# A two-layer graph network on one core: the second layer's preparation spread over 27 units, its first weight factor on ScalarE, and f1, f2 taken from the turning products

## The chip, the core and the metric

The kernel runs on one core of a Trainium2 chip. The metric is the device time of one execution in microseconds. The kernel before takes 3600.33 us in the median of three runs (3599.05 to 3604.43); the profiled execution spans 3601.0 us.

## What is computed

Sixteen graphs of N = 1024 nodes with F = 256 features pass through two layers. Each layer ends with a residual sum and a layer norm. Layer 0 is an attention layer with batch norms and is not touched here. Layer 1, for each of H = 4 heads, is

```
fts    = inputs @ W[h]
f1, f2 = fts @ w1[h] + b1[h], fts @ w2[h] + b2[h]
logits = f1[:, None] + f2[None, :]
coefs  = a*softmax(leaky_relu(logits, 0.2) + bias_mat) + (1-a)*softmax(adj)
out    = elu(coefs @ fts + bias[h] + inputs)
x      = layernorm(inputs + mean of out over heads)
```

`bias_mat` is -1e9 where there is no edge, so the first softmax needs only neighbours. The exponential of a leaky ReLU of a sum is the larger of two products: exp(f1 + f2) and exp(0.2 (f1 + f2)). Divided by exp(0.2 f1), which cancels in the softmax, a weight is max(exp(0.8 f1) exp(f2), exp(0.2 f2)): `A` holds the first factor per target row, and two columns behind the features in each source row's table hold the other two.

## The kernel before, in words

Layer 0 runs first, up to 799.4 us. It leaves the hidden features turned around, features over partitions, in `h_dram`. The adjacency stands in `adj16` as bf16.

Layer 1 uses that most columns of the adjacency are empty in a given block of 128 rows. Per graph the nodes are in K = 8 blocks. For each block `it` of target rows the used source nodes are collected into chunks of 128; `CAPS` says how many chunks each block may need (6, 4, 3, 3, 3, 3, 2, 2, together 26). A chunk's feature rows `xc` and mask columns `mc` are fetched by indirect DMA from GpSimd's queue. `weights` makes the 128 x 128 weights of the four heads from them, and PE multiplies.

Two things are therefore done per graph:

*Preparation* (class `Graph`). `load_mask`, `load_h`, `load_x` bring the data in. `counts`, `used`, `places`, `placed`, `mark`, `pick`, `indices` find which source goes to which chunk. `elu`, `turn`, `residual`, `means`, `norm`, `scale` finish layer 0's output and its layer norm. `shares1` multiplies `h` with `WW` to give f1 and f2, and `factors` makes their exponentials. `table` and `spread` write the row table and the factors of f1 to DRAM. `split`, `total`, `mask`, `neighbours`, `summed`, `shares` make the second softmax, which has only two values per row, from a plain product with the adjacency (block `mr` per row block, in `fp32r`).

*Units* (class `Unit`), 16 per graph, one for a row block and a pair of heads. `gather` (PE, L1389) multiplies chunks into `pu`; `share` (ScalarE) starts `s` with the second softmax; `mix` (DVE, L1405 to L1409) adds the first; `turn` and `turned` transpose `s` (PE, then ScalarE); `linear` (PE, L1429) multiplies by W1 into `pv`; `addends` (GpSimd, L1376) adds bias and input; `add`, `exps`, `sum`, `power`, `close` finish with the ELU, the mean over heads and the layer norm.

The order within each engine is the order in which the Python code calls these steps, since everything is inside `tc.manual_schedule()`: there is no planner, and each engine works through its queue in order. The main loop runs over `n`, and calls for each `n` the steps of units at fixed distances behind (`linear` of unit n - 2, `mix` of n - 1, `add` of n - 3). Preparation steps are hung into this loop by `side(g)`: `first[i]` runs just ahead of `mix`, `after[i]` at the end of unit i, mostly while the graph before computes its units. A step's PE part stands in `first[i]` and its DVE part in `after[i]` of the same unit, as here:

```
first[8] += [g.pick, g.shares1]
after[8] += [g.indices, g.factors]
```

Graph 0's preparation has no units to stand beside and is written out ahead of the loop. Buffers matter for the steps below: `pv` (L1426) has one PSUM buffer, `pu` two, the preparation's PSUM tag `s` two, the chunks' `xc` and `mc` 17 each.

Of the kernel before, what the change touches and what calls it, by code (L numbers as in the profile page):

```python
# [8 lines left out]
F32 = mybir.dt.float32  # L9
# [10 lines left out]
P = 128  # L20
# [7 lines left out]
def kernel(  # L28
# [83 lines left out]
    mt_dram = [dpool.tile([N + 1, N], BF16, name=f"mt_dram_{i}") for i in range(2)]  # L112
# [16 lines left out]
    with tc.tile_pool(name="ipool", bufs=1) as ipool:  # L129
# [14 lines left out]
        for i in range(2):  # L144
            nc.gpsimd.dma_start(xe_dram[i][N : N + 1, :], zero[:, 0:XW])
            nc.gpsimd.dma_start(mt_dram[i][N : N + 1, :], zero)
# [890 lines left out]
    with ExitStack() as l1:  # L1037
        xpool = l1.enter_context(tc.tile_pool(name="x1pool", bufs=2))
# [5 lines left out]
        ps_s = l1.enter_context(tc.tile_pool(name="ps_s", bufs=2, space=PSUM))  # L1044

        class Graph:
# [7 lines left out]
            def load_mask(self):  # L1054

                b = self.b
                if b in ready1:
                    self.mt = ready1[b]
                else:
                    self.mt = m1pool.tile([P, K, N], BF16, tag="mt", name=f"mt1_{b}")  # L1060
                    nc.sync.dma_start_transpose(self.mt, adj16[b])
                self.rw = pk.tile([P, K, N], BF16, tag="rw", name=f"rw_{b}", bufs=1)
                nc.sync.dma_start(self.rw, adj16[b].rearrange("(q p) j -> p q j", p=P))
# [14 lines left out]
            def counts(self):  # L1078

                self.pc = ps_s.tile([P, K, K], F32, tag="s", name=f"pc_{self.b}")  # L1080
                for k in range(K):
                    for q in range(K):
                        nc.tensor.matmul(
                            self.pc[:, k, q : q + 1], self.rw[:, q, k * P : (k + 1) * P],
                            ones16[:, 0:1], start=True, stop=True,
                        )

            def used(self):

                self.act = pk.tile([P, K, K], BF16, tag="act", name=f"act_{self.b}", bufs=2)  # L1090
                nc.vector.tensor_scalar(self.act, self.pc, 1.0, None, ALU.min)
# [14 lines left out]
            def placed(self):  # L1106

                b = self.b
                pos = pk.tile([P, K + 1, K], F32, tag="pos", name=f"pos_{b}", bufs=1)
                nc.scalar.copy(pos, self.pp)  # L1110
                nc.vector.tensor_tensor(most, most, pos[:, K, :], ALU.max)
                pi = pk.tile([P, K, K], I32, tag="pi", name=f"pi_{b}", bufs=1)
                nc.vector.tensor_copy(pi, pos[:, 0:K, :])
                nc.vector.tensor_scalar(pi, pi, P - 1, None, ALU.bitwise_and)
                self.r16 = pk.tile([P, K, K], FP16, tag="r16", name=f"r16_{b}", bufs=2)
                nc.vector.tensor_copy(self.r16, pi.rearrange("p k q -> p q k"))
                nc.vector.tensor_tensor(pos[:, 0:K, :], pos[:, 0:K, :], pi, ALU.subtract)
# [3 lines left out]
                    t, pos[:, 0:K, :].rearrange("p k q -> p (k q)").unsqueeze(2).to_broadcast([P, K * K, n]),  # L1121
# [7 lines left out]
                self.oh = pk.tile([P, K, P, K], FP16, tag="rw", name=f"oh_{b}", bufs=1)  # L1129

            def mark(self, q):
                nc.vector.tensor_tensor(
                    self.oh[:, q], iota16, self.r16[:, q, :].unsqueeze(1).to_broadcast([P, P, K]),
                    ALU.is_equal,
                )

            def pick(self):

                self.pl = ps_s.tile([P, NC], F32, tag="s", name=f"pl_{self.b}")
                n = max(CAPS)  # L1140
                for q in range(K):
                    for k in range(K):
                        nc.tensor.matmul(  # L1143
                            self.pl[:, CAT[q] : CAT[q] + CAPS[q]],
                            self.oh[:, q, :, k], self.t16[:, k, q * n : q * n + CAPS[q]],
# [3 lines left out]
            def store_mask(self):  # L1149
                nc.sync.dma_start(  # L1150
                    mt_dram[self.b % 2][0:N, :].rearrange("(k p) i -> p k i", p=P), self.mt
                )

            def indices(self):

                b = self.b
                self.ix = pk.tile([P, NC], U32, tag="ix", name=f"ix_{b}", bufs=2)
                self.im = pk.tile([P, NC], U32, tag="im", name=f"im_{b}", bufs=2)
                nc.vector.tensor_scalar(self.ix, self.pl, float(N), None, ALU.add)
                nc.vector.scalar_tensor_tensor(self.im, self.pl, float(K), row8, ALU.mult, ALU.add)  # L1160

            def fetch_rows(self, c):

                self.xc[c] = pk.tile([P, XW], F32, tag="xc", name=f"xc_{self.b}_{c}", bufs=17)
# [5 lines left out]
            def fetch_mask(self, c):  # L1170

                self.mc[c] = pk.tile([P, P], BF16, tag="mc", name=f"mc_{self.b}_{c}", bufs=17)
                nc.gpsimd.indirect_dma_start(  # L1173
                    out=self.mc[c], out_offset=None,
                    in_=mt_dram[self.b % 2].rearrange("n (q i) -> (n q) i", i=P),
# [10 lines left out]
            def weights(self, c):  # L1186

                it = max(q for q in range(K) if CAT[q] <= c)
                w = self.w[c] = pk.tile([P, H, P], F32, tag="w", name=f"w_{self.b}_{c}", bufs=12)
                xc = self.xc[c]  # L1190
                for h in range(H):
                    nc.vector.tensor_scalar(  # L1192
                        w[:, h, :], self.A[it][:, h, :], xc[:, F1 + h : F1 + h + 1],
                        xc[:, F1 + H + h : F1 + H + h + 1], ALU.mult, ALU.max,
                    )
                nc.vector.tensor_tensor(  # L1196
                    w, w, self.mc[c].unsqueeze(1).to_broadcast([P, H, P]), ALU.mult
                )

            def elu(self, oc):  # L1200

                hv = self.h[:, oc, :]
                m = pk.tile([P, N], F32, tag="hm", name=f"hm_{self.b}_{oc}", bufs=1)
                nc.scalar.activation(
                    m, hv, AF.Exp, bias=t3[:, oc : oc + 1], scale=s3[:, oc : oc + 1]
# [4 lines left out]
                nc.vector.scalar_tensor_tensor(hv, m, 1.0, hv, ALU.min, ALU.max)  # L1210

            def turn(self, k):
                pz = self.pz[k] = ps_s.tile([P, F], F32, tag="s", name=f"pz_{self.b}_{k}")
                for oc in range(C):
                    nc.tensor.transpose(
                        pz[:, oc * P : (oc + 1) * P], self.h[:, oc, k * P : (k + 1) * P], ident
                    )

            def residual(self, k):
                xk = self.x[:, k, 0:F]  # L1220
                nc.vector.tensor_tensor_reduce(
                    out=xk, in0=self.pz[k], in1=xk, scale=1.0, scalar=0.0,
                    op0=ALU.add, op1=ALU.add, accum_out=self.mv[:, 0, k : k + 1],
                )

            def shares1(self):

                self.pf = ps_s.tile([P, K, 2 * H], F32, tag="s", name=f"pf_{self.b}")
                for k in range(K):
                    for oc in range(C):  # L1230
                        nc.tensor.matmul(  # L1231
                            self.pf[:, k, :], self.h[:, oc, k * P : (k + 1) * P], WW[:, oc, :],
                            start=(oc == 0), stop=(oc == C - 1),
                        )

            def means(self):

                nc.vector.tensor_scalar(self.mv[:, 0], self.mv[:, 0], -1.0 / F, None, ALU.mult)
                for k in range(K):
                    d = pk.tile([P, F], BF16, tag="d", name=f"d_{self.b}_{k}", bufs=2)  # L1240
# [4 lines left out]

            def norm(self):
                self.rs = pk.tile([P, 3, K], F32, tag="rs", name=f"rs_{self.b}", bufs=2)
                rs = self.rs
                nc.vector.tensor_scalar(self.mv[:, 1], self.mv[:, 1], 1.0 / F, None, ALU.mult)
                inv_std(rs[:, 1, :], self.mv[:, 1, :], rs[:, 0, :])  # L1250
                nc.vector.tensor_tensor(rs[:, 2, :], self.mv[:, 0], rs[:, 1, :], ALU.mult)
# [8 lines left out]
            def factors(self):  # L1260
# [3 lines left out]
                nc.vector.tensor_tensor(self.f, self.pf, xw[:, b], ALU.add)  # L1264
# [6 lines left out]
                f2 = self.f[:, :, H : 2 * H]  # L1271
                nc.vector.memset(self.x[:, :, F : F + 1], 1.0)
                nc.scalar.activation(self.x[:, :, F1 : F1 + H], f2, AF.Exp)
# [12 lines left out]
            def split(self, k):  # L1286

                if k == 0:
                    self.xs = pk.tile([P, K, 2, F2], F32R, tag="xs", name=f"xs_{self.b}", bufs=1)
                    nc.vector.memset(self.xs[:, :, 0, F:F2].bitcast(F32), 1.0)  # L1290
                xk = self.x[:, k, 0:F]
                nc.scalar.copy(self.xs[:, k, 0, 0:F], xk)
                nc.vector.tensor_tensor(  # L1293
                    self.xs[:, k, 1, 0:F], xk, self.xs[:, k, 0, 0:F].bitcast(F32), ALU.subtract
                )

            def total(self):

                b = self.b
                px = ps_s.tile([P, F], F32, tag="s", name=f"pX_{b}")  # L1300
                for k in range(K):
                    for part in range(2):
# [3 lines left out]
                        )  # L1306
                self.X = pk.tile([P, F], F32, tag="X", name=f"X_{b}", bufs=2)
                nc.scalar.copy(self.X, px)
                self.deg = pk.tile([P, K], F32, tag="deg", name=f"deg_{b}", bufs=2)

            def mask(self, it):

                self.mr[it] = pk.tile([P, K, P], F32R, tag="mr", name=f"mr_{self.b}_{it}", bufs=3)
                nc.gpsimd.dma_start(self.mr[it], self.mt[:, :, it * P : (it + 1) * P])  # L1314
# [14 lines left out]
            def summed(self, it):  # L1329
                b, pm = self.b, self.pm[it]  # L1330
                self.S[it] = pk.tile([P, F], F32, tag="S", name=f"S_{b}_{it}", bufs=K + 1)
# [333 lines left out]
```

## Time and profile before

| stretch, us from the start | what it holds | length |
|---|---|---|
| 0 to 799.4 | layer 0 | 799.4 |
| 799.4 to 913.9 | graph 0's preparation, to the first `mix` | 114.5 |
| 913.9 to 1075.7 | graph 0's units | 161.8 |
| 1075.7 to 3484.2 | units of graphs 1 to 14, each with the next one's preparation | 14 x 172.0 |
| 3484.2 to 3601.0 | units of graph 15 | 116.8 |

A stretch begins with the first L1405 of a graph: DVE runs that line once per unit. Over the whole span PE is busy for 78%, DVE for 77%, GpSimd for 39% and ScalarE for 37%. Where two engines are each busy for four fifths and neither is full, the average doesn't tell what bounds: one has to ask, inside one such stretch, who waits for whom. A group of the profile gives busy time and the mean duration of one instruction; because instructions of one engine overlap, the distance from start to start is often shorter than the duration. An fp32 product on PE appears as two records, a transpose as one.

### The profile page before, as it was taken

Reading aid. Unit: us, or ns where it says so; the run is one execution under the profiler, and the core shown is the slowest. Engines: PE = TensorE matmul, PEld = TensorE weight load, DVE = VectorE, ACT = ScalarE, POOL = GpSimd, SP = SyncE. Lnnn points to the kernel's source line nnn. Section 1 sums busy time; section 2 is a strip of 40 time slices with the busy share of each in tenths; the row PEclk is TensorE's granted clock in tenths of the full one; section 3 lists DMA queues with packets and bytes.
Section 4 is the critical chain, followed back from the end, with each engine's and each line's share of the span. In section 5 each row is a group of like instructions: output and inputs, shape, how many; then the busy total and the mean of one; then the engine's idle time right before and its main releaser. Section 6 shows DMA issues by size and latency. Waiting matters only on the chain.

```text
span 3601.0 us, 45794 instructions
## 1 busy us (share of the span) xinstructions
PE 2810.2 (78%) x15591; PEld 2233.4 (62%) x15591; DVE 2777.1 (77%) x6820; ACT 1319.3 (37%) x2484; POOL 1392.6 (39%) x1425
## 2 busy tenths in 40 slices
PE   7936999985787777787877777787778787877786
PEld 6723444434676666675766666676667576766675
DVE  4369999953877878787878787868787877878788
ACT  1247777742233232333332323233333332332323
POOL 0010000004454545453535454454545454545462
PEclk9957999996887979898879888888888897989898
DMA  9797985537473746464646475655556564746441
GB/s 278 210 268 152 240 207 158 158 106 150 125 146 93 151 100 142 103 153 90 151 92 158 88 171 91 150 94 146 104 134 120 130 134 109 151 99 143 102 86 35
DMA packets 647283, 496.53 MB, mean 138 GB/s; under 512 B 286680, under 2 KB 567296, under 8 KB 640896
## 3 DMA queue, kind: packets, MB, share of 16 engines
q1 hardware_dynamic: 462656, 320.18, 32.1%
q0 software_dynamic: 183168, 170.81, 27.6%
q8 instruction: 127, 2.08, 0.2%
q10 hardware_dynamic: 1216, 2.51, 0.2%
q14 instruction: 116, 0.95, 0.1%
HBM read 291.09 MB, written 135.21 MB: 118 GB/s over the span
## 4 chain that ended last, share of the span: by engine, by line
DVE 32%; PE 12%; issue 9%; DMA 9%; POOL 6%; ACT 6%; SPq 2%; another core or an unknown queue 1%; DVEq 0%; POOLq 0%; ACTq 0%
DVE w L1192 8%; PE pv L1429 4%; DMA A<-a_dram 4%; DVE w L1196 3%; PE pf L1231 3%; DVE v L1436 3%; DMA mc<-mt_dram,im 2%; DVE s L1409 2%; DVE xs L1293 2%; POOL v L1376 2%; ACT d L1241 2%; POOL mc L1173 2%; PE pl L1143 2%; DVE v L1449 2%; DMA mr<-mt 2%
## 5 line engine op out<-in xcount | busy, mean ns | idle before, releaser
L1429 PE MATMUL pv<-W1s,sT 128*128 128x256 f32 x2048 | 659.2, 479 | 566.9 <-DVE z L1405 432.8
L1429 PEld LDWEIGHTS pv<-W1s,sT 128*128 128x128 f32 x2048 | 469.1, 238 | 716.7 <-issue 478.5
L1389 PE MATMUL pu<-xc,w 128*128 128x257 f32 x3328 | 821.2, 400 | 11.3 <-DVE w L1196 9.1
L1389 PEld LDWEIGHTS pu<-xc,w 128*128 128x128 f32 x3328 | 656.6, 204 | 104.9 <-DVE w L1196 12.2
L1192 DVE TENSOR_SCALAR w<-A,xc 128x128 f32<-128x128 f32 x1664 | 508.3, 376 | 54.0 <-DMA A<-a_dram 54.0
L1376 POOL TENSOR_TENSOR v<-x,bias 128x512 f32<-128x512 f32 x256 | 301.1, 1176 | 495.1 <-DVE acc L1447 311.0
L1165 POOL DMA_INDIRECT xc<-xe_dram,ix x416 | 417.9, 1005 | 144.0 <-issue 123.8
L1173 POOL DMA_INDIRECT mc<-mt_dram,im x416 | 426.0, 1024 | 104.9 <-issue 100.1
L584 PE MATMUL pa<-em,wh 128*128 128x512 f32 x1024 | 451.2, 598 | 18.9 <-issue 13.4
L584 PEld LDWEIGHTS pa<-em,wh 128*128 128x128 f32 x1024 | 193.5, 192 | 251.6 <-issue 235.7
L1472 ACT ACTIVATE o<-o,ors 128x256 f32<-128x256 f32 x128 | 76.8, 600 | 739.0 <-DVE ors L1469 556.6
L1440 ACT ACTIVATE m<-v,neg 128x512 f32<-128x512 f32 x256 | 184.8, 722 | 395.2 <-DVE z L1405 293.7
L1196 DVE TENSOR_TENSOR w<-w,mc 128x512 f32<-128x512 f32 x416 | 317.0, 762 | 14.2
L1324 PE MATMUL pm<-xs,mr 128*128 128x256 f32 (+1 forms) x2048 | 282.8, 294 | 36.0 <-DMA mr<-mt 35.6
L1324 PEld LDWEIGHTS pm<-xs,mr 128*128 128x128 f32 x2048 | 265.5, 196 | 43.6 <-issue 37.0
L1409 DVE SCALAR_TENSOR_TENSOR s<-pu,z,s 128x256 f32<-128x256 f32 x512 | 224.2, 479 | 22.3 <-ACT m L1440 0.5
L1399 ACT ACTIVATE s<-S,q 128x256 f32<-128x256 f32 x512 | 228.3, 493 | 1.2 <-DVE q L1350 1.2
L1423 ACT COPY sT<-pt 128x512 f32<-128x512 f32 x256 | 147.5, 576 | 121.2 <-PE pt L1417 119.0
L1463 POOL TENSOR_TENSOR ors<-ors,mhalf 128x1 f32<-128x1 f32 x128 | 72.8, 569 | 300.3 <-DVE ors L1469 284.6
L1314 POOL DMA_DIRECT2D mr<-mt x128 | 121.0, 947 | 166.2 <-PE pm L1324 139.7
L1447 DVE SCALAR_TENSOR_TENSOR acc<-m,v 128x512 f32<-128x512 f32 x128 | 87.8, 686 | 125.9 <-ACT m L1440 125.9
L540 ACT ACTIVATE e<-eb,c,s 128x1024 f32<-128x1024 f32 x128 | 155.0, 1236 | 79.0 <-DVE sm L554 42.7
(259 smaller groups left out, 4014.0 us busy)
## 6 DMA issues: line engine op xcount, KB each, us to landing
mr<-mt POOLq DMA_DIRECT2D x128, 512.0 KB
x<-in_x_dram SPq DMA_DIRECT2D x32, 1024.0 KB
adj<-in_adj_dram POOLq DMA_DIRECT2D x16, 2048.0 KB
rw<-adj SPq DMA_DIRECT2D x16, 2048.0 KB
mt_dram<-mt SPq DMA_DIRECT2D x16, 2048.0 KB
A<-a_dram SPq DMA_DIRECT2D x128, 256.0 KB
xe_dram<-x SPq DMA_DIRECT2D x16, 1060.0 KB
wh_dram<-wx SPq DMA_DIRECT2D x16, 1024.0 KB
```

Source lines behind the costliest of these rows:

```text
L584: nc.tensor.matmul(acc[b, hf, oc], wh[b][:, k, oc * P : (oc + 1) * P], ems[b, k][:, hf * HALF : (hf + 1) * HALF], start=(k == 0), stop=(k ...
L1165: nc.gpsimd.indirect_dma_start(out=self.xc[c], out_offset=None, in_=xe_dram[self.b % 2], in_offset=bass.IndirectOffsetOnAxis(ap=self.ix[:, ...
L1173: nc.gpsimd.indirect_dma_start(out=self.mc[c], out_offset=None, in_=mt_dram[self.b % 2].rearrange("n (q i) -> (n q) i", i=P), in_offset=ba ...
L1192: nc.vector.tensor_scalar(w[:, h, :], self.A[it][:, h, :], xc[:, F1 + h : F1 + h + 1], xc[:, F1 + H + h : F1 + H + h + 1], ALU.mult, ALU.max,)
L1196: nc.vector.tensor_tensor(w, w, self.mc[c].unsqueeze(1).to_broadcast([P, H, P]), ALU.mult)
L1324: nc.tensor.matmul(pm[:, 0:n], lhsT, self.xs[:, k, part, 0:n], start=(k == 0 and part == 0), stop=(k == K - 1 and part == 0),)
L1376: nc.gpsimd.tensor_tensor(self.v2, self.g.x[:, self.it, 0:F].unsqueeze(1).to_broadcast([P, HP, F]), bias1[:, h : h + HP, :], ALU.add,)
L1389: nc.tensor.matmul(self.pu[:, hh, 0:F1], g.w[c][:, h, :], g.xc[c][:, 0:F1], start=(c == cs[0]), stop=(c == cs[-1]),)
L1399: nc.scalar.mul(self.s[:, hh], g.S[it], g.q[:, it, h0 + hh : h0 + hh + 1])
L1409: nc.vector.scalar_tensor_tensor(s[:, hh], self.pu[:, hh, 0:F], z[:, hh : hh + 1], s[:, hh], ALU.mult, ALU.add)
L1429: nc.tensor.matmul(self.pv[:, hh, :], self.sT[:, hh, fc, :], W1s[:, fc, self.hp * HP + hh, :], start=(fc == 0), stop=(fc == C - 1),)
L1440: nc.scalar.activation(self.m, self.v2, AF.Exp, bias=neg1, scale=1.0)
```

## The change

It has five parts.

1. The plan. The preparation now spans units -27 to 8 of its graph instead of -2 to 15 of the graph before, and has three lists: `early` (DVE work right after `mix`), `first` (PE work after `linear`), `after` (ScalarE, DMA and GpSimd work, at the unit's end). A PE step stands in `first[n]` and the step that uses its result in `early[n + 1]`, a unit later. The units' own steps are spaced likewise: `turn` is at n - 2, `linear` at n - 3, `add` and `exps` at n - 4, the final store at n - 8. The written-out prologue goes; the loop starts at n = -27.
2. Weights. `larger` multiplies `A` by the first exponential on ScalarE, and `weights`, a unit later, does maximum and mask on DVE in one operation per head. Before, DVE did one `tensor_scalar` per head (L1192) and one `tensor_tensor` per chunk for the mask (L1196).
3. f1, f2. `turn` is a product with `IW`, the identity with WW's eight columns behind it, so that f1 and f2 come out beside the turned features; `shares1` goes (L1231).
4. `mix` takes z in two operations instead of three, with the reciprocal of alpha (`ial_bc`) prepared once.
5. Buffers and paths. `rw` and its one-hot successor `oh` are handled in halves; `mr` is loaded from the mask in DRAM instead of SBUF (three `mt_dram`); `xc` and `mc` have 15 buffers, x three, `s` three, `m` two; `deg` is copied on DVE instead of ScalarE; `shares` is done in three parts.

The diff, cut to its core:

```diff
-            def weights(self, c):
-
+            def larger(self, c):
                 it = max(q for q in range(K) if CAT[q] <= c)
                 w = self.w[c] = pk.tile([P, H, P], F32, tag="w", name=f"w_{self.b}_{c}", bufs=12)
-                xc = self.xc[c]
                 for h in range(H):
-                    nc.vector.tensor_scalar(
-                        w[:, h, :], self.A[it][:, h, :], xc[:, F1 + h : F1 + h + 1],
-                        xc[:, F1 + H + h : F1 + H + h + 1], ALU.mult, ALU.max,
-                    )
-                nc.vector.tensor_tensor(
-                    w, w, self.mc[c].unsqueeze(1).to_broadcast([P, H, P]), ALU.mult
-                )
+                    nc.scalar.mul(w[:, h, :], self.A[it][:, h, :], self.xc[c][:, F1 + h : F1 + h + 1])
+
+            def weights(self, c):
+                for h in range(H):
+                    nc.vector.scalar_tensor_tensor(
+                        self.w[c][:, h, :], self.w[c][:, h, :],
+                        self.xc[c][:, F1 + H + h : F1 + H + h + 1], self.mc[c], ALU.max, ALU.mult,
+                    )
...
             def turn(self, k):
-                pz = self.pz[k] = ps_s.tile([P, F], F32, tag="s", name=f"pz_{self.b}_{k}")
+
+                pz = self.pz[k] = ps_s.tile([P, C, TW], F32, tag="s", name=f"pz_{self.b}_{k}")
                 for oc in range(C):
-                    nc.tensor.transpose(
-                        pz[:, oc * P : (oc + 1) * P], self.h[:, oc, k * P : (k + 1) * P], ident
+                    nc.tensor.matmul(
+                        pz[:, oc, :], self.h[:, oc, k * P : (k + 1) * P], IW[:, oc, :],
+                        start=True, stop=True,
                     )
...
             def mask(self, it):

                 self.mr[it] = pk.tile([P, K, P], F32R, tag="mr", name=f"mr_{self.b}_{it}", bufs=3)
-                nc.gpsimd.dma_start(self.mr[it], self.mt[:, :, it * P : (it + 1) * P])
+                nc.gpsimd.dma_start(
+                    self.mr[it],
+                    mt_dram[self.b % 3][0:N, it * P : (it + 1) * P].rearrange("(k p) i -> p k i", p=P),
+                )
...
+            def turned(n, f, then, *args):
+                first[n] += [each(f, *args)]
+                early[n + 1] += [each(then, *args)]
+
+            after[-27] += [g.load_mask]
+            after[-26] += [each(g.load_rows, 0)]
+            after[-25] += [g.load_h]
+            after[-23] += [g.store_mask, each(g.load_rows, 1)]
+            turned(-24, g.counts, g.used, 0)
+            turned(-20, g.counts, g.used, 1)
+            turned(-19, g.places, g.placed)
...
+            turned(-12, g.pick, g.indices, 0)
+            turned(-9, g.pick, g.indices, 1)
...
+            for k, n in enumerate((-17, -16, -15, -15, -14, -14, -13, -13)):
+                turned(n, g.turn, g.residual, k)
...
+            turned(-3, g.total, g.totalled)
+            for it, n in enumerate((-2, -2, -1, 0, 4, 5, 6, 7)):
+                turned(n, g.neighbours, g.summed, it)
...
+                        after[-5 + 2 * it + j] += [each(g.fetch_mask, c), each(g.fetch_rows, c)]
+                        after[-3 + 2 * it + j] += [each(g.larger, c)]
+                        early[-2 + 2 * it + j] += [each(g.weights, c)]
...
-            for n in range(len(units) + 6):
-                b, i = divmod(n, NU)
-                do(n - 3, "add")
-                do(n - 2, "turned")
-                do(n - 4, "power")
-                do(n, "addends")
-                if n < len(units):
+            for n in range(-EARLY, len(units) + 9):
+                do(n - 2, "turn", "turned")
+                if 0 <= n < len(units):
                     units[n].gather(0)
                     units[n].gather(1)
-                do(n - 2, "linear")
-                stand(0, b, i)
-                do(n - 1, "mix", "turn")
...
+                do(n - 1, "sums")
+                do(n - 4, "add")
+                do(n - 1, "invert")
+                do(n - 7, "offset")
+                do(n - 1, "mix")
+                do(n - 4, "exps")
+                stand(0, n)
                 do(n, "share")
-                do(n - 3, "sum")
-                do(n - 5, "close")
-                stand(1, b, i)
+                do(n - 3, "linear")
+                stand(1, n)
+                do(n - 4, "sum")
+                stand(2, n)
+                do(n - 2, "addends")
+                do(n - 5, "power")
+                do(n - 7, "close")
+                do(n - 8, "store")
```

## The prediction

> **What bounds the kernel now.** I looked for the repeating stretch first. The first L1405 of each graph (one per unit, so a clock for the units) comes at 913.9, 1075.7, 1248.2 ... 3484.2 us: 162 us for the first graph and then 172.0 us each, 10.75 us per unit. [...]So 2,570 of the 3,601 us are fifteen almost equal stretches, and a change to them counts fifteen times.
>
> The table by stretch (length; busy time of PE, PEld, DVE, ACT, POOL; granted clock; DMA share; GB/s) for two graphs in the middle and for the last:
>
> ```profile
> 1937.40:2108.10 170.70, 132.07 (x775) 114.03 (x774) 134.68 (x366) 54.14 (x123) 84.87 (x86) 0.87 0.58 124
> 2108.10:2279.30 171.20, 131.11 (x776) 113.31 (x774) 135.11 (x366) 54.21 (x123) 85.16 (x86) 0.86 0.56 124
> 3484.20:3601.00 116.80, 82.16 (x367) 67.44 (x365) 98.20 (x260) 38.90 (x76) 43.88 (x47) 0.89 0.17 41
> ```
>
> No engine fills the 171 us: DVE and PE are busy for 135 and 132 and idle for 36 and 39. The last graph, with no successor to prepare, needs 55 us less, although the preparation's own groups (oh, xs, S, x, h and small ones; pm, pf, pl, pz, pX, pc, pp) come to only 28 us of DVE and 40 of PE, on two engines that could work at once: it is placed badly rather than too large. The waits of the same graph say how (engine, line, releaser; us, times, longest):
>
> ```profile
> PEld pv L1429 <- issue: 31.2, 8, 6.7
> PE pv L1429 <- DVE z L1405: 28.2, 8, 6.3
> ...
> PEld pv L1429 <- ACT sT L1423: 9.4, 4, 5.2
> ...
> DVE acc L1447 <- ACT m L1440: 7.8, 2, 4.2
> ...
> DVE f L1264 <- PE pf L1231: 6.1, 1, 6.1
> ...
> DVE mv L1249 <- ACT d L1241: 4.1, 1, 4.1
> ```
>
> PE waits at the linear step for DVE (28 us), then DVE waits inside the same unit for what PE or ScalarE has only just begun. The two take turns. The chain of waits shows the worst unit pair, end to end:
>
> ```profile
> 2005.14 4.05 ACT d L1241 x16
> 2009.67 1.67 POOL rs L159
> 2011.53 0.60 DVE v L1436
> 2012.28 3.75 PE pv L1429 x8
> 2016.03 3.79 PE pl L1143 x64
> 2019.82 6.85 PE pf L1231 x32
> ```
>
> **What the Trainium skill says.** "SBUF — State Buffer", Who interferes with whom: DVE operations in a two-port mode, such as tensor_scalar, hold a port pair exclusively against GpSimd; DVE operations with two SBUF inputs contend only with GpSimd's SBUF reads. The trace agrees in kind: L1192 takes 328 ns at least, 341 in the median and 2,083 at most. "TensorE: Matmul & The Clock Gate", What's actually happening: the array falls to half clock after an idle window of about 3.4 us and recovers when busy. The trace grants only 0.86 to 0.87 here, with PE holes of 3 to 5 us. "ScalarE: Activation LUTs", What ACT_TABLE_LOAD costs: 186 ns + 0.833 ns per element, 93 more per pointer operand, 93 overlapped back to back: 0.40 us for 256 elements. L1399 starts its next 0.40 us later.
>
> **The change part by part,** per graph. Prices are start to start, from the instructions by time:
>
> ```profile
> 1938.81 1.89 PE L1429 MATMUL pv<-W1s,sT 128*128 128x256 f32 x8
> 1940.53 0.60 PE L1417 MATMUL pt<-ident,s 128*128 128x128 f32 x4
> 1940.97 3.63 PE L1389 MATMUL pu<-xc,w 128*128 128x257 f32 x16
> ```
> ```profile
> 2039.89 0.87 DVE L1409 SCALAR_TENSOR_TENSOR s<-pu,z,s 128x256 f32<-128x256 f32 x2
> 2040.68 1.11 DVE L1192 TENSOR_SCALAR w<-A,xc 128x128 f32<-128x128 f32 x4
> 2041.82 0.69 DVE L1196 TENSOR_TENSOR w<-w,mc 128x512 f32<-128x512 f32 x1
> 2042.43 0.68 DVE L1449 SCALAR_TENSOR_TENSOR v<-m,v 128x512 f32<-128x512 f32 x1
> ```
>
> *Weights.* Removed from DVE: 104 of L1192 (30.4 us in this graph) and 26 of L1196 (0.61 apart unhindered, 0.75 on the mean: 16 to 19.5, say 17.5). Added: 104 scalar_tensor_tensor of 128 elements, a form the trace lacks. L1409 has a pointer too and costs (2040.68 - 2039.89)/2 = 0.40 for 256 elements; without pointer L1332 is 0.34 for 256 and L1447 0.60 for 512, so 128 elements fewer are 0.13 less: 0.27 with a pointer, 0.21 without. I take 0.26: 27 us. DVE gains 21 (18 to 28). ScalarE gains 104 products of 128 elements at 0.40 - 0.11 = 0.29, 30 us, and goes from 54 to about 85 of busy time: beside DVE and PE, so free unless late.
>
> *f1, f2.* L1231 goes: 32 records, 6.85 us (two records per fp32 product). L1215's 16 transposes at 0.11 (1.8 us) become 32 records of 144 columns. Between 144 columns at L1389's rate (0.12) and the weight-load pitch of L1231 (0.214), I take the latter: 6.85. PE gains 1.8. DVE copies out 8 small pieces, each priced like L1405's 0.15: +1.2.
>
> *Small DVE edits.* L1407 gone, 16 x 0.20 = -3.2; deg copied on DVE, 8 x 0.15 = +1.2; shares in three parts, 12 more operations of 0.16 to 0.20, +2.2; one more addition, +0.2. With the +1.2 above DVE ends at 134.7 - 21 + 1.6 = 115 us.
>
> *PE sum at full clock.* L1389 208 x 0.216 = 45.0; L1429 128 x 0.215 = 27.5; L1417 64 x 0.11 = 7.0; neighbours 128 x 0.12 = 15.4; turning 6.85; pick 3.8; total, counts, places 5.5: 111 us.
>
> *GpSimd.* An indirect DMA holds it 1.0 us and 0.30 us of issue, so 52 x 1.28 + 8 masks x 1.27 + 16 additions x 1.17 + powers 7 = 102 us. Unchanged, now third in line. Masks come from DRAM instead of SBUF: same 256-byte pieces, hidden by at least a unit.
>
> *The plan.* Each result is used a unit later, so the waits above lose their cause. One unit's PE and DVE work still cannot drift far apart: pv has one buffer, so linear waits for add in the same unit. I spread both sums over the 16 units by the written plan (gather 0.87 us per chunk; linear and turn 2.2; counts 0.85 a half; neighbours 2.0; turning 0.85; pick 1.9 a half. DVE z, mix, add and acc 2.4 in even units, with the eight closing operations of the second pair 4.8 in odd ones; weights 1.05 per chunk; a mark 0.75, a residual with its copy 0.5, an elu half 0.6, a low part 0.4, placed 2.7, a row block's sum 0.5):
>
> PE 10.2, 9.1, 7.3, 7.3, 8.7, 6.8, 6.8, 8.7, 5.7, 4.8, 4.8, 4.8, 4.8, 7.2, 7.9, 6.8
> DVE 6.3, 8.7, 6.3, 7.0, 5.5, 8.2, 6.7, 7.4, 6.1, 6.1, 5.4, 7.8, 5.0, 6.7, 8.3, 11.3
>
> (The second row sums to 113; the stretch's overlaps make up the rest.) The larger of each pair sums to 124 us, the estimate for lockstep; perfect smoothing gives 115. To 124 I add 4 for the clock (PE is the larger in eight pairs, 65 us; at an expected 0.93 these grow by 7%) and 5 for GpSimd's additions meeting two-input DVE work (DVE instructions that overran their form's shortest by over 0.15 us did so by 12 us per graph, mostly beside L1376; more operations now have two inputs). That is 133.
>
> *Ends.* The prologue loses its 25 us hole (DVE idle 855.5 to 880.7, masks queued behind 19 fetches), as only three row blocks are needed before the first unit; but fetches of 15 us still follow the table, and rw is now loaded in halves. I take first L1405 at 885 instead of 914 (870 to 910). The last graph has half its neighbours still to do, yet lighter weights: 108 instead of 117.
>
> Sum: 885 + 15 x 133 - 5 (graph 14 prepares one graph less) + 108 = 2,983, say 2,985 us.
>
> **The rivals.** *Better overlap*, 118 per graph: 885 + 1,770 - 5 + 105 = 2,755. For it: DVE 115, PE 111. Against: all three engines near their sum, and DVE and GpSimd exclude each other. *A new wait takes part back*, 150 to 160 per graph, 3,240 to 3,390. ScalarE is in order, and its first factor now waits for a fetched chunk two units after issue, with exps and turned queued behind; DMA share rises from 0.58 to about 0.75 when the same bytes go in 133 us. Units 11 and 12 ask 10 us each of GpSimd for six chunks. *Slower*: if each half row block pays a landing on the path (the chain has pieces of 4.5 to 6.4 us of DMA for mc and xc), with ScalarE's 1.2 us per chunk, 124 + 16 x 3.5 = 180 per graph, 885 + 2,700 - 5 + 110 = 3,690. Against it: fetches are two units, some 16 us, ahead, and 15 buffers hold exactly what the plan keeps alive.
>
> **How the numbers follow.** Forecast (125 to 145 per graph, 2,850 to 3,160) 0.62; better 0.12; part taken back 0.19; slower 0.06; within 0.2% 0.01. The range cuts off about a tenth on each side: 2,830 is 123 per graph, 3,260 is 151. Everything but the last two cases is faster: 0.93.
>
> **What would show it.** Right: L1405's successor every 133 us; PE waits at linear under 10 us per graph; no DVE wait for pf or squares; DVE near 115, ACT near 85; clock 0.92 or more; new weights 0.26 apart. Wrong: ScalarE waiting for xc or A by DMA; PE waiting for mr; GpSimd without idle time; clock still 0.87, which alone would make PE 128 us.

## The result and the profile after

The changed kernel takes 2912.53 us in the median (2909.76 to 2914.03) against 3599.69 before (3598.91 to 3604.43), a ratio of 0.8088, 95% interval 0.8074 to 0.8102. The forecast was 2,985.

The clock for the units is now line L1460, once per unit on DVE. Its first instance of each graph comes at 884.9, 1017.1, 1144.0, 1271.1 ... 2677.4, 2795.6 us: 132.2 for the first graph, then 126.9 to 129.2 each (mean 127.7 over graphs 2 to 12, against 172.2 for the same graphs before), 118.2 for graph 14, and 115.1 after the last. The table by stretch, for two graphs in the middle and the last (length; busy time of PE, PEld, DVE, ACT, POOL; granted clock; DMA share; GB/s):

```profile
1653.70:1781.80 128.10, 112.73 (x759) 98.61 (x758) 118.01 (x358) 84.89 (x221) 89.38 (x85) 0.99 0.77 167
1781.80:1908.90 127.10, 114.00 (x759) 99.83 (x758) 118.08 (x359) 84.89 (x221) 89.32 (x85) 0.97 0.78 168
2795.60:2910.70 115.10, 87.80 (x447) 75.03 (x445) 97.13 (x268) 58.53 (x140) 55.73 (x56) 0.93 0.28 56
```

DVE idles 10 us of a graph instead of 36, PE 13 to 15 instead of 39. PE's busy time fell by 18 us although its work hardly changed, and the clock rose from 0.87 to 0.98. The waits of the first of these graphs (engine, line, releaser; us, times, longest):

```profile
PEld pv L1491 <- DVE v L1498: 17.3, 10, 3.3
...
PE pv L1491 <- DVE v L1498: 13.3, 9, 2.9
POOL xc L1193 <- DMA xe_dram<-x: 9.5, 1, 9.5
DVE v L1498 <- POOL v L1430: 6.6, 2, 3.3
```

DVE's waits for pf and for the squares are gone. PE's wait at the linear step is halved. The profile now names `add` (DVE v) as its releaser, where before it named the first operation of `mix` (DVE z). That need not be a new wait: by the program `linear` waits for the one buffer of `pv`, which `add` frees, and in the kernel before z stood directly behind `add` in DVE's queue and started 0.08 us before `add` ended, too close for the profile to tell them apart. What is new is that `add` in turn sometimes waits for GpSimd. Where that happens, the chain of waits runs through GpSimd's queue:

```profile
1740.12 0.94 POOL xc L1193
1741.08 1.29 POOL v L1430
1742.37 0.02 issue
1742.39 0.69 DVE v L1498
...
1750.12 0.94 POOL xc L1193
1751.06 0.03 issue
1751.09 1.28 POOL v L1430
1752.37 0.02 issue
1752.39 0.70 DVE v L1498
```

The addition of bias and input (L1430) stands behind fetches in GpSimd's queue; the fetches had stood still for 9.5 us until the row table reached DRAM, and then ran one behind the other.

The two prices that the trace of before did not have, from PE and DVE by time:

```profile
1659.06 1.09 PE L1249 MATMUL pz<-IW,h 128*128 128x136 f32 x8
```
```profile
1755.94 4.80 DVE L1224 SCALAR_TENSOR_TENSOR w<-w,xc,mc 128x128 f32<-128x128 f32 x12
```

Turning with f1 and f2 costs 0.116 us from start to start. The weights cost 0.263 undisturbed; these twelve took 4.80 us instead of 3.2, because the eighth lasted 1.85 us instead of 0.34, beside a GpSimd addition from 1758.19 to 1759.47.

### The profile page after: what moved, and what is told of

Same layout as the page of the kernel before. It is cut to its first block, busy times and chain, and to the rows that moved or that the text cites. A ratio compares the mean times of both kernels' runs of the same rounds, so it can differ in the third digit from the quotient of the medians.

```text
span 2910.7 us, 46981 instructions
## 1 busy us (share of the span) xinstructions
PE 2511.2 (86%) x15335; PEld 2001.6 (69%) x15335; DVE 2506.6 (86%) x6698; ACT 1811.4 (62%) x4068; POOL 1464.5 (50%) x1426
## 4 chain that ended last, share of the span: by engine, by line
DVE 42%; issue 17%; PE 16%; DMA 12%; POOL 8%; ACT 4%; SPq 0%; DVEq 0%; POOLq 0%; ACTq 0%
DVE w L1224 12%; DMA xe_dram<-x 5%; PE pa L585 4%; PE pw L302 4%; DVE v L1498 4%; DVE s L1470 3%; POOL xc L1193 3%; PE pv L1491 2%; DVE v L1512 2%; POOL mc L1201 2%; DVE oh L1153 2%; DMA xc<-xe_dram,ix 2%; DVE o L1514 2%; DVE v L1511 2%; POOL v L1430 2%
## 5 line engine op out<-in xcount | busy, mean ns | idle before, releaser
L1443 PE MATMUL pu<-xc,w 128*128 128x257 f32 x3328 | 777.4, 385 | 0.0
L1491 PE MATMUL pv<-W1s,sT 128*128 128x256 f32 x2048 | 523.7, 401 | 186.1 <-DVE v L1498 182.8
L1491 PEld LDWEIGHTS pv<-W1s,sT 128*128 128x128 f32 x2048 | 393.3, 198 | 294.3 <-DVE v L1498 239.9
L1193 POOL DMA_INDIRECT xc<-xe_dram,ix x416 | 460.4, 1107 | 265.1 <-DMA xe_dram<-x 141.7
L1220 ACT ACTIVATE w<-A,xc 128x128 f32<-128x128 f32 x1664 | 512.0, 388 | 60.0 <-DMA xc<-xe_dram,ix 39.1
L1224 DVE SCALAR_TENSOR_TENSOR w<-w,xc,mc 128x128 f32<-128x128 f32 x1664 | 534.8, 390 | 10.5 <-ACT w L1220 10.5
L1430 POOL TENSOR_TENSOR v<-x,bias 128x512 f32<-128x512 f32 x256 | 305.1, 1192 | 10.0 <-DVE z L1460 4.8
L1498 DVE TENSOR_TENSOR v<-pv,v 128x512 f32<-128x512 f32 x256 | 174.6, 682 | 86.4 <-POOL v L1430 82.8
L1362 POOL DMA_DIRECT2D mr<-mt_dram x128 | 122.8, 959 | 96.1 <-PE pm L1375 83.1
L545 ACT ACTIVATE e<-e,v,u 128x1024 f32<-128x1024 f32 x128 | 152.3, 1229 | 22.7 <-DVE e L544 16.6
L1479 PE MATMUL pt<-ident,s 128*128 128x128 f32 x1024 | 159.6, 279 | 2.5 <-ACT sT L1485 2.5
```

The lines of the kernel that those rows point to most:

```text
L1193: nc.gpsimd.indirect_dma_start(out=self.xc[c], out_offset=None, in_=xe_dram[self.b % 2], in_offset=bass.IndirectOffsetOnAxis(ap=self.ix[:, ...
L1220: nc.scalar.mul(w[:, h, :], self.A[it][:, h, :], self.xc[c][:, F1 + h : F1 + h + 1])
L1224: nc.vector.scalar_tensor_tensor(self.w[c][:, h, :], self.w[c][:, h, :], self.xc[c][:, F1 + H + h : F1 + H + h + 1], self.mc[c], ALU.max, ...
L1430: nc.gpsimd.tensor_tensor(self.v2, self.g.x[:, self.it, 0:F].unsqueeze(1).to_broadcast([P, HP, F]), bias1[:, h : h + HP, :], ALU.add,)
L1443: nc.tensor.matmul(self.pu[:, hh, 0:F1], g.w[c][:, h, :], g.xc[c][:, 0:F1], start=(c == cs[0]), stop=(c == cs[-1]),)
L1491: nc.tensor.matmul(self.pv[:, hh, :], self.sT[:, hh, fc, :], W1s[:, fc, self.hp * HP + hh, :], start=(fc == 0), stop=(fc == C - 1),)
```

## The experiments

A period is the time from the first L1460 of a graph (or the line that stands for it) to that of the next, as a mean over graphs 2 to 12 of the profiled execution. The changed kernel has 127.7, the kernel before 172.2. The edits are shown shortened: "..." stands for lines or arguments left out, and long names are cut to their last part.

### Plan and weights apart

The new plan with the old weights:

```diff
             def larger(self, c):
-                for h in range(H):
-                    nc.scalar.mul(w[:, h, :], self.A[it][:, h, :], ...)
...
             def weights(self, c):
                 for h in range(H):
-                    nc.vector.scalar_tensor_tensor(w, w, xc, mc, ALU.max, ALU.mult)
+                    nc.vector.tensor_scalar(w, A, xc, xc, ALU.mult, ALU.max)
+                nc.vector.tensor_tensor(w, w, mc, ALU.mult)
```

> The new plan with the old weights: per chunk four tensor_scalar and one tensor_tensor on DVE, nothing on ScalarE. Theory (placement gave most of the gain; the weights gave DVE room of about 20 us): DVE about 137 us per graph, ScalarE about 55, and since DVE is then the largest sum and the stretch was 10 us above the largest sum before, 140 to 150 per graph instead of 127.6, 3,110 to 3,260 us in all. Rival (the weights are the main cause, and the plan alone is worth little): 160 per graph or more, 3,420 us or more.

Measured: 3152.45 us, ratio 0.8753 (0.8738 to 0.8767), period 143.4, DVE 139.

The kernel before with the new weights alone, ScalarE's part at the start of the unit in which DVE does the rest:

```diff
                 do(n - 2, "turned")
+                for s, at in ((b + 1, i), (b, NU + i)):
+                    if s < B:
+                        made(graphs[s], at, "larger")
```

> The kernel before with the new weights alone: the first factor on ScalarE at the start of the unit in which DVE takes maximum and mask. Theory (the waits of PE and DVE on each other set the 172 us): a part of the 20 us of DVE comes through, because the weights lie between mix and exps inside the wait loop: 155 to 170 per graph, 3,320 to 3,570 us. Rival (DVE's work sets the time, whatever the plan): 150 per graph or less, below 3,280 us.

Measured: 3438.87 us, ratio 0.9543 (0.9527 to 0.9559), period 162.6. One stretch of each, the new weights alone first:

```profile
1712.50:1874.10 161.60, 127.79 (x777) 111.44 (x776) 117.87 (x340) 83.92 (x227) 87.23 (x85) 0.87 0.60 131
```
```profile
1604.50:1748.00 143.50, 120.10 (x761) 103.26 (x761) 138.94 (x385) 55.69 (x118) 89.12 (x86) 0.94 0.68 149
```

The first has DVE's busy time of the changed kernel, 118 us, and still needs 161.6: over graphs 2 to 12 the weights took 16 us from DVE (135.2 to 119.3) and 9.6 came through. The second has more DVE work than the kernel before and is 28.8 us shorter, with DVE full to 97%. So everything but the weights (the plan, with f1 and f2, `mix` and the buffers) is worth 28.8 us per graph with the old weights and 34.9 with the new; the weights are worth 9.6 without the rest and 15.7 with it. The saving isn't quite the same, though: with the rest the weights take 20 us from DVE (138.7 to 118.3).

And a part of the 6 us that did not come through is this experiment's own. Among the waits in its stretch stands

```profile
DVE w L1194 <- ACT w L1190: 10.4, 2, 7.2
```

DVE waits for ScalarE's factor, 10.6 us per graph over graphs 2 to 12; the changed kernel, which makes the factor a unit earlier, does not have this wait there. The old plan with the factor a unit earlier was not run. So that work taken from an engine pays more once that engine no longer waits is only in part shown; what the second run shows plainly is that the plan pays by itself: DVE has more work than before, and the period is 28.8 us shorter.

### Which part of the plan

The consumer of each PE result of the preparation back in the same unit:

```diff
             def turned(n, f, then, *args):
                 first[n] += [each(f, *args)]
-                early[n + 1] += [each(then, *args)]
+                after[n] += [each(then, *args)]
```

> The changed kernel with the consumer of each of the preparation's PE results put back to the end of the same unit instead of the next unit's start, all else as changed. Theory (the unit of distance removes waits of DVE for PE): DVE waits for pm, pl, pz and pc come back, 1 to 2 us in each of some 18 places but partly hidden by the lead of DVE: 132 to 142 per graph, 2,980 to 3,140 us. Rival (the distance is not needed; what helped was spreading over 27 units and putting linear and add apart): within 1% of the changed kernel, 2,885 to 2,940 us.

Measured: 2934.56 us (2923.72 to 2943.62), ratio 0.8138 (0.8118 to 0.8158), period 129.9. The rival: about 2 us of the 44 per graph. DVE waits 5.8 us for pm again, and that is nearly all of its waits for PE.

The units' own steps back at their old distances, the preparation as changed:

```diff
-                do(n - 2, "turn", "turned")
+                do(n - 3, "add")
+                do(n - 2, "turned")
                 ...
-                do(n - 1, "sums")
-                do(n - 4, "add")
-                do(n - 1, "invert")
                 do(n - 7, "offset")
-                do(n - 1, "mix")
-                do(n - 4, "exps")
+                do(n - 1, "sums", "invert", "mix")
+                do(n - 3, "exps")
                 stand(0, n)
                 do(n, "share")
-                do(n - 3, "linear")
+                do(n - 2, "linear")
                 stand(1, n)
-                do(n - 4, "sum")
+                do(n - 1, "turn")
+                do(n - 3, "sum")
```

> The changed kernel with the units' own steps at their old distances: linear two units behind instead of three, add, exps and sum three instead of four, turn right behind mix at the end of the unit's PE work; preparation and weights as changed. Theory (putting turn, linear and add a unit further apart is what removed PE's waits for DVE z and v, 28 us before): 140 to 155 per graph, 3,100 to 3,330 us. Rival (the preparation's spread over 27 units did it): within 2% of the changed kernel, 2,860 to 2,970 us.

Measured: 3138.91 us, ratio 0.8718 (0.8704 to 0.8733), period 142.7. The wait of PE for DVE is back, and a second one with it:

```profile
PE pv L1491 <- DVE z L1460: 18.3, 6, 6.5
...
DVE v L1498 <- POOL v L1430: 16.1, 5, 5.9
```

So this order costs 15.0 us per graph. Not all of that is the distance of the kernel before, though: the second wait is new. GpSimd's addition is called at n - 2 and `add` here at n - 3, one unit later; in the changed kernel it is two units, in the kernel before three, and there DVE had no such wait. So 15.0 is an upper bound for the distance between turn, linear and add alone; a version with the addition called earlier was not run.

With the new weights in both, the way from 162.6 to 127.7 is up to 15.0 for that order, about 2 for the preparation's consumers a unit later, and by subtraction about 18 for the rest: the spread over 27 units, the buffers, `mix`, f1 and f2. Each was taken out alone, so these shares need not add up.

### f1 and f2

```diff
-                    nc.tensor.matmul(pz[:, oc, :], self.h[...], IW[:, oc, :], start=True, stop=True)
+                    nc.tensor.transpose(pz[:, oc * P : (oc + 1) * P], self.h[...], ident)
...
+            first[-10] += [g.shares1]
```

> The changed kernel with f1 and f2 taken again from 32 records of a separate product one unit ahead of their use, and plain transposes. Theory: PE gets about 5 us per graph more (6.85 for the product and 1.8 for the transposes against 3.7 for the combined product), DVE 1.4 less; PE's sum of 113 reaches 118, and the units in question are not PE's longest, so plus 1 to 3 per graph, 2,925 to 2,960 us. Rival (PE is the bound): plus 5 per graph, 2,985 us or more. Second rival (GpSimd and DVE are the bound): same time within 0.3%.

Measured: 2984.99 us, ratio 0.8287 (0.8273 to 0.8301), period 132.5. The result is the rival's, but the assumption under all three was wrong. The product costs 3.76 us here, not 6.85: 32 records 0.112 apart. With 2.30 for the transposes against 3.68 for the combined product, PE's own work grows by 2.4 us, and PE's busy time by 5 (114 to 119 over graphs 2 to 12), because linear, neighbours and total also got longer at a lower clock (0.92 to 0.95). The granted clock explains the old price. Before, at the linear step after a wait of 6.3 us and at the product, and then the product in this experiment:

```profile
2012.28:2016.03 3.75, 3.75 (x12) 2.84 (x13) 3.65 (x9) 1.40 (x3) 3.13 (x3) 0.50 1.28 181
...
2019.82:2026.67 6.85, 6.85 (x33) 6.85 (x34) 0.41 (x4) 0.60 (x1) 3.76 (x5) 0.50 0.23 64
```
```profile
1730.85:1734.48 3.63, 3.63 (x34) 3.63 (x33) 3.52 (x8) 0.00 (x0) 3.31 (x3) 1.00 0.15 9
```

At half the clock the same 32 records take nearly twice the time. The Trainium skill ("TensorE: Matmul & The Clock Gate", What's actually happening) gives half clock after an idle window of about 3.4 us. The linear step fits that: PE had waited for 6.3 us. The product does not. These two stretches lie just ahead of it and over it:

```profile
2016.22:2019.63 3.41, 3.41 (x60) 3.41 (x60) 3.24 (x7) 0.00 (x0) 2.80 (x3) 1.00 1.24 166
2019.63:2026.67 7.04, 7.04 (x37) 7.04 (x36) 0.56 (x5) 0.60 (x1) 3.95 (x5) 0.50 0.22 62
```

PE was busy throughout, with 60 records of 2 to 6 columns each (L1143), and the clock fell all the same; over the product's records of 8 columns it stayed low. The measurement decides: a PE that shows as busy can fall to half clock when its records are this narrow. It also answers in part why the clock fell in this experiment. From 900 us on its clock falls 41 times, and 9 of these falls come after 3.41 us in which PE was busy throughout, with 20 to 26 records of this product among them; the changed kernel has 20 falls, none of them after such a stretch. The other 32 come after stretches in which PE was busy for at most 0.65 of the time. That it is the few columns that count is inferred; no run varied them alone.

### Which engine counts now

PE relieved, by leaving the low half out of the neighbours' product (the second softmax uses the rounded parts alone):

```diff
-                    for part in (0, 1) if k < K - 1 else (1, 0):
+                    for part in (0,):
```

> The changed kernel with the low half left out of the neighbours' product (the second softmax then uses only the rounded high parts): 64 of 128 records of 0.12 us fewer, 7.7 us of PE per graph, in the unit pairs 14, 15, 0 and 4 to 7. The separate product of f1 and f2 had added 5 us to PE and about as much to the period. Theory A (PE sets the period, with DVE close behind): 4 to 7.7 us per graph less, 2,790 to 2,850 us. Theory B (PE and DVE take turns unit by unit, so that both count where they are the longer): 2 to 4 less, 2,850 to 2,880. Theory C (GpSimd and the units without neighbours set it): under 1.5 less, above 2,890.

Measured: 2868.0 us, ratio 0.7967 (0.7953 to 0.798), period 124.4: 3.3 us for 7.7 of work, theory B.

DVE relieved, by leaving out the ELU's operations. There are four of them per graph, 2.4 us in all, where the expectation counts eight:

```diff
-                early[-22 + n] += [each(g.elu, n // 2, n % 2)]
```

> The changed kernel without the eight half-column operations of layer 0's ELU (its minimum and maximum are left out, layer 1 then starts from the linear part): 8 times 0.6, 4.8 us of DVE per graph less, in units 10 to 13 of the graph before. Theory A (PE alone sets the period): under 1 us per graph, above 2,895 us. Theory B (they take turns): 2 to 4 us less, 2,850 to 2,885 us. Theory C (DVE is the bound): 4.8 less, 2,840.

Measured: 2909.12 us (2904.4 to 2910.27), ratio 0.8079 (0.8064 to 0.8094), period 127.4: 0.3 us per graph for 2.4 us of work, where theory B, halved with the work, asks for 1 to 2. DVE's busy time fell from 118.0 to 116.3, and over graphs 2 to 12 its wait for GpSimd at `add` grew from 5.9 to 7.3 us per graph. So DVE's work is not the bound in units 10 to 13, where it was taken out; the run says little on the others.

GpSimd relieved, its addition replaced by a fill (the last ELU's argument lacks bias and input):

```diff
-                nc.gpsimd.tensor_tensor(self.v2, self.g.x[...], bias1[...], ALU.add)
+                nc.gpsimd.memset(self.v2, 0.0)
```

> The changed kernel with GpSimd's addition of bias and input to each unit replaced by a fill with zero (the ELU's argument then lacks bias and input): one fill of 512 elements per unit instead of an addition with two SBUF inputs. DVE instructions overrun their form's shortest by 12.5 us per graph now. Theory (the overruns are DVE waiting out GpSimd's reads, and DVE counts in the period): overruns fall to 3 or less, DVE from 118 to 108, 3 to 8 us per graph less, 2,785 to 2,865 us. Rival (overruns come from GpSimd's descriptor writing or other traffic): overruns stay above 9, same time within 1%. Second rival (overruns go, PE takes the time): overruns fall, time falls by under 2 us per graph.

Measured: 2787.27 us, ratio 0.7744 (0.773 to 0.7758), period 119.8. The overruns, by which DVE instructions took over 0.15 us longer than the shortest of their form, are 0.5 us per graph instead of 12.5. One stretch:

```profile
1611.00:1731.20 120.20, 112.42 (x759) 100.19 (x758) 105.83 (x359) 84.45 (x221) 78.58 (x86) 0.97 0.83 178
```

That the overruns are DVE waiting out GpSimd's additions is shown: all 96 of them in eight graphs of the changed kernel overlap one, and a fill, which reads nothing, causes almost none. It agrees with the Trainium skill ("SBUF — State Buffer", Who interferes with whom): two-input DVE operations contend with GpSimd instructions that read SBUF, not with those that only write. But the fill is also shorter (0.54 us against 1.28), so this run does not tell what these hold-ups (the next expectations call them the lock) cost from what GpSimd's queue costs.

### The order in GpSimd's queue

```diff
-                stand(2, n)
                 do(n - 2, "addends")
+                stand(2, n)
```

> The changed kernel with GpSimd's addition for unit n - 2 called ahead of the unit's fetches and mask loads instead of behind them. With the addition replaced by a fill the period fell by 7.9 us, from 127.7 to 119.8, and DVE's overruns from 12.5 to 0.5 us per graph; DVE's waits for GpSimd at add stayed at 6.4. Theory (the lock on the SBUF port costs, the order in the queue does not): DVE's 6.6 us of waits at add go, but the overruns stay at 12 and PE hides the rest: 0 to 2 us per graph less, 2,880 to 2,913 us. Rival (the waits at add are on the path): 5 us or more per graph less, below 2,835 us.

Measured: 2876.16 us (2874.46 to 2883.53), ratio 0.7988 (0.7974 to 0.8003), period 125.5. That is 2.2 us per graph, just above the theory's 0 to 2 and far from the rival's 5; DVE's waits at `add` for GpSimd are gone, and the overruns stay at 11.5.

The same, and the row table a unit earlier:

```diff
-            after[-7] += [g.table]
+            after[-8] += [g.table]
```

> The changed kernel with GpSimd's additions ahead of the fetches and the row table written one unit earlier. With the additions ahead alone the period is 125.5 us, and GpSimd still waits 10 us in unit 11 for the table and then works through the fetches without a pause while units 13 and 14 take 13.6 and 12.9 us. Theory (the late table pushes the fetches, ScalarE's first factors and DVE's weights of units 12 to 14 back; a unit earlier it does so less): 1 to 3 us per graph less, 2,830 to 2,862 us. Rival (units 13 and 14 are long because DVE has 11 us of work in each, whatever the fetches do): same time, 2,865 to 2,885 us.

Measured: 2794.55 us (2793.84 to 2797.99), ratio 0.7762 (0.7751 to 0.7772), period 120.4, more than the theory gave. GpSimd's wait for the table is gone, and unit 13 takes 8.6 us instead of the 13.6 of the run before. One stretch, and PE's wait at the linear step in it:

```profile
1606.10:1726.40 120.30, 114.27 (x759) 100.83 (x758) 116.61 (x358) 84.37 (x222) 89.55 (x85) 0.96 0.79 178
...
PE pv L1491 <- DVE v L1498: 5.4, 5, 3.0
```

The overruns are still 12.3 us per graph. So order alone, with the hold-ups in place, gives 7.3 us, about as much as the fill with its 7.9. These need not be the same microseconds: the fill ran with the old order, and order and fill together were not tried, so what the hold-ups cost the period in this order stays open. This version beats both kernels, by 4% of the changed one's time.

### The addition moved to PE

The bias as three bf16 pieces on three rows, added by PE into pv, the input as the second operand of DVE's `add`; and then the same with the earlier table. The edit also leaves v two buffers instead of four.

```diff
+                    nc.tensor.matmul(
+                        self.pv[:, hh, :], ones16[0:3, :], bias3[:, self.hp * HP + hh, :],
+                        start=True, stop=False,
+                    )
...
-                nc.vector.tensor_tensor(self.v2, self.pv, self.v2, ALU.add)
...
+                nc.vector.tensor_tensor(self.v2, self.pv, x, ALU.add)
...
-                do(n - 2, "addends")
```

> The changed kernel without GpSimd's addition: the bias, in three bf16 pieces on three rows, is added by PE into pv (32 records of 256 columns in bf16 per graph, about 0.12 us each, 3.8 us), and DVE's add takes the input row block itself as its second operand, at the same size. Theory (the lock and GpSimd's queue were worth 7.9 us per graph, and PE's own work is passed on nearly whole, as the separate product of f1 and f2 showed with 4.8 us of period for 5 of work): 127.7 - 7.9 + 3.8 = 123 to 125 per graph, 2,835 to 2,870 us, overruns under 1 us. Rival (PE's added work falls into units where it waits anyway): 120 per graph, 2,790 us.

> The same with the row table written one unit earlier, right behind the last scale. Theory (GpSimd's wait of 9 to 13 us for the table, followed by a burst of fetches, delays DVE's weights in units 13 and 14 little once the additions are out of its queue): 0 to 2 us per graph less than with the bias on PE alone. Rival (the burst is what makes these units 12 us long): 3 us or more per graph less, about 50 us in all.

Measured: 3063.18 us in the median of five executions (3038.64 to 3082.39; a sixth took 3088.92), ratio 0.8499 (0.8466 to 0.8532), and 3041.86 us (3039.14 to 3045.8), ratio 0.8446 (0.8432 to 0.846): both far slower than the changed kernel, a plain miss of both theory and rival. The earlier table gave about 1.4 us per graph ((3063.18 - 3041.86) / 15), as its theory had it, but the first version's times lie further apart than that. In the second the overruns are zero and DVE needs only 106 us, but PE rose from 114 to 126 of a period of 135. Its own new group, over 400 us:

```profile
L1490 PE MATMUL pv<-bias,ones 3*128 3x256 bf16 x94 | 26.2, 278 | 1.9 <-issue 1.9
```

From start to start one takes 0.208 us at a granted clock of 1.00, not 0.12: 6.7 us per graph. Linear, total and neighbours grew by 5, and a further 6 us are idle time in the product that finds places (pp), with no releaser that the profile shows. Why is open, and whether the fewer buffers of v play a part was not tried. The runs show only that in this place 6.7 us of records cost the period 14.9 us, against the version of 120.4 that has the addition on GpSimd.

## Why the prediction was right, and where not

**The mechanism held in the main.** PE and DVE took turns, a plan with more distance stopped most of that, and of the 20 us that the weights took from DVE 15.7 then came through. The step "Each result is used a unit later, so the waits above lose their cause" did not tell its members apart, though: the preparation's results need the extra unit little (2 us per graph), the units' own turn, linear and add need it more (up to 15, part of which is the wait for GpSimd's addition).

**The period, 133 = 124 + 4 + 5, measured 127.7.** Fifteen of them were 79 us too long, and the last graph took 7 of these back: that is the forecast's error of 72. Each term was off:
- *124 for lockstep, the larger of each unit's pair.* Too large: with queue order mended the period is 120.4, hold-ups and clock included. So the larger of the pair is no floor, presumably because buffers let one engine run ahead. PE also entered it too heavy, at a half-clock price for the turning; with the measured price the pairs sum to 122.
- *4 for the clock at 0.93.* It was 0.97 over graphs 2 to 12, which by the same sum is 2. PE's holes of 3 us and more went with the waits.
- *5 for GpSimd's additions beside two-input operations.* The overruns are there, 12.5 us against 12 before. What they cost the period by themselves was not measured: the fill took them away together with some of GpSimd's time.
- *Missing: GpSimd's queue.* I called GpSimd "unchanged, now third in line" and put its six chunks per unit only under a rival. The late table and the additions behind the fetches cost 7.3 us per graph. The terms that were too high hid the omission: without it they would have missed by 12.6 us per graph, not by 5.3. That the sum came this near is in part luck.

**Prices.** New weights 0.26, measured 0.263; with their share of overruns 32 us per graph, not 27, which is more than DVE's 118 against 115. ScalarE 85, as predicted; after the first graph its new factor waited only for A, at most 2.4 us per graph. Turning at 0.214 from L1231's pitch, measured 0.116: I took a half-clock price for a property of the weight load. The duration was right, the granted clock of its stretch (0.50) was left out of account. So f1 and f2 with the turning took 5.7 us from PE (9.4 to 3.7), not 1.8.

**PE waiting at linear under 10 us:** 13.3, half the old 28.2. The wait I had not seen in it is `add` behind GpSimd; with the order mended it is 5.4.

**Ends.** First line of the clock at 884.9, predicted 885. Graph 14 gave back 9, not 5. The last graph took 115.1, not 108: DVE works for 97 us of it, and PE still waits 9.2 us for `add` at the linear step.

**Rivals.** *Part taken back* did not come: neither ScalarE nor the transfers held up the queue, DMA share 0.77 as expected. *Better overlap* at 118 was held unlikely because of "all three engines near their sum"; the reordered version at 120.4 shows that most of it was there. *Slower* had no sign of itself: fetches two units ahead were enough outside units 11 to 14.

## What to carry to other kernels

When two engines take turns, put distance between the dependent steps of the same unit before taking work off an engine: here the plan gave 28.8 us with more work on DVE, while 16 us less work for DVE without the plan gave 9.6, with a new wait of DVE for ScalarE beside it. Read the granted clock of the stretch before taking a duration from it as a price. After such a change, look at the queue of the engine that was third in line: work that somebody waits for should not stand behind transfers that wait for a table.

## What the runs showed of the hardware

- In the kernel before, the granted clock was 0.50 over the product of f1 and f2 (0.51 in one of the sixteen graphs), and its records of 8 columns came every 0.213 us; at a clock of 1.00 it was 0.112 us.
- PE need not be idle for the clock to fall: in eight of the sixteen graphs of the kernel before it fell at the end of 3.41 us in which PE was busy throughout, nearly all of it with records of 2 to 6 columns.
- Beside a GpSimd addition with two SBUF inputs a two-input DVE instruction of 128 elements took 1.85 us instead of 0.34; with a GpSimd fill of the same size in its place such overruns came to 0.5 us per graph in all, against 12.5.
- A bf16 record with 3 rows and 256 columns took 0.208 us from start to start among fp32 products at full clock, about what an fp32 record of 256 columns takes (0.216). Neither the few rows nor the type shortened it here; why is not shown.
